# Layer 0 of a graph network: where the value sums live, when keys are asked for, and how many steps the next queries wait

## The chip, the cores and the metric

The kernel runs on one core of one Trainium2 chip. Its time is the time of one execution on the device in microseconds (us), the median of the runs. Smaller is better. The engines are TensorE (PE, with weight loads shown apart as PEld), VectorE (DVE), ScalarE (ACT), GpSimd (POOL) and SyncE (SP), whose queue issues nearly all transfers.

## The reference, cut to what matters

Four residual layers, each followed by a layer norm, run over 3327 nodes with 256 features and one adjacency matrix. The change touches layer 0 only:

```python
Qn = _cos_normalize(features @ Wq.T)          # x / max(|x|, 1e-4)
Kn = _cos_normalize(features @ Wk.T)
att = jnp.where(adj > 0, Kn @ Qn.T, NEG)
att = jax.nn.softmax(att, axis=1)
prop_fea = att @ features
...
x = _layernorm(x + _L0_gnn_ref(x, adj, Wq, Wk))
```

Layers 1 to 3 are graph attention layers of the same shape (masked scores, softmax, times values). The kernel runs them as five further passes over the same adjacency mask.

## The kernel before, in words

The nodes are padded to 3328, which is NT = 26 tiles of 128. One side of the attention matrix is cut into NB = 7 blocks of 512 columns (the last has 256). The other side is walked in 26 tiles. The main loop is a list of steps (layer, block b, tile j). In step j the loop makes the weights of a tile two steps ahead (`make_to`), and multiplies the weights of tile j with the values of tile j into accumulators `po`, which stand for the whole block.

To make one tile of weights in layer 0 (`weights0`), TensorE multiplies keys and queries into a PSUM bank `ps` (L455), ScalarE takes the exponential `ex` with the key's reciprocal length `rq` as its scale (L464), and VectorE multiplies by the mask into `e` (L444). Every second step also turns a pair of adjacency tiles into a mask (`take_adj`: ScalarE `pos` L407 and `mask` L408) and counts them (VectorE `acc` L416).

Block 0 uses plain products, eight matmul records of 257 columns in a step (L1271). Blocks 1 to 5 use a Strassen form (L726) that handles two tiles at once and needs sums of values. `combine` computes those sums in block 0, one pair of tiles p in step p + 9, with four VectorE subtractions (L656 to L659) and a column of ones set by GpSimd (L655). It writes them to DRAM with a transfer on SP (L660), and `fetch_tsum` streams them back for each later block (L664).

Keys come from `keys0`: a product `pq` (L305), then the square and a copy on ScalarE (L312, L313), then column sums `pn` on TensorE (L317), then the reciprocal root on VectorE (L322 and the lines of `rsqrt`). It is a generator, and one part of it runs in a step.

The queries of the next block come from `queries0(b + 1)`, also a part in a step: products `pk` (L335) and a copy (L343), then four squares with sums on ScalarE (L350), then `lengths` on GpSimd (L296 and `rsqrt`, 15 small instructions), then four scalings `kr` on ScalarE (L362), then four transposes `pkT` on TensorE (L366) and a copy (L367). In blocks 1 to 5 these parts are called in steps j = 10, 11, 12, 13 and 14; in block 0 in steps 18 to 22. The closing of the block before (`finish`) is spread over the first dozen steps of each block, most of it on VectorE.

The first four steps are emitted in written order on TensorE, ScalarE, VectorE and GpSimd. After that a scheduler sets the order of every engine: it plays the program through with modelled times, and an engine that is free in that play takes, among what is ready, the instruction that was written first. On the chip each engine keeps the order so found, and waits at the head of its queue for what is late.

Tiles come from rings of buffers. `x4k` (two buffers) holds `xT`, the pieces of the transposed input, and before the change also the sums of block 0. `tsum` (three buffers) holds the sums that come back. The PSUM banks for everything but `po` are a ring of three, and `e` has five.

Of the kernel before, what the change touches and what calls it, by code (L numbers as in the profile page):

```python
# [14 lines left out]
ALU = mybir.AluOpType  # L15
# [6 lines left out]
H = 128  # L22
# [5 lines left out]
COS_EPS = 1e-4  # L28
# [5 lines left out]
def gnn_stack(ctx: ExitStack, tc: tile.TileContext, a: dict, N: int, out: bass.AP):  # L34
# [8 lines left out]
    nc = tc.nc  # L43
# [6 lines left out]
    def bw(b):  # L50
        return min(CH, NP - b * CH)

    def tiles_of(b):
        return range(4 * b, min(4 * b + 4, NT))
# [11 lines left out]
    def bank(name):  # L66
        return ps_b.tile([P, CH], F32, tag="pb", name=name)
# [16 lines left out]
    n = 1  # L84
# [7 lines left out]
    for k in range(4):  # L92
# [5 lines left out]
    V = [  # L98
        [big.tile([P, D + 1], F32, name=f"v{i}_{t}") for t in range(NT)]
        for i in range(2)  # L100
    ]
# [30 lines left out]
    def rsqrt(dst, v, n, eng=nc.vector, tag="rs"):  # L132

        g = cols.tile([P, n], I32, tag=tag + "_g", name="rs_g")
        eng.tensor_scalar(g, v.bitcast(I32), -0.5, MAGIC, ALU.mult, ALU.add)
        y = g.bitcast(F32)
        vh = cols.tile([P, n], F32, tag=tag + "_v", name="rs_v")
        eng.tensor_scalar(vh, v, -0.5, None, ALU.mult)
        for k in range(3):
            q = cols.tile([P, n], F32, tag=tag + "_q", name="rs_q")  # L140
            eng.tensor_tensor(q, y, y, ALU.mult)
            eng.tensor_tensor(q, q, vh, ALU.mult)
            z = dst if k == 2 else cols.tile([P, n], F32, tag=tag + "_y", name="rs_y")
            if eng is nc.vector:
                eng.scalar_tensor_tensor(z, q, 1.5, y, ALU.add, ALU.mult)
            else:
                eng.tensor_scalar(q, q, 1.5, None, ALU.add)
                eng.tensor_tensor(z, q, y, ALU.mult)
            y = z
# [125 lines left out]
    def load_xT(g):  # L275
        wd = bw(g)
        xT = work.tile([P, 2, CH], F32, tag="x4k", name="xT", bufs=2)
        src = a["xT"].rearrange("(h p) n -> p h n", p=P)
        if g == 0:
            for q, c in ((nc.scalar, 0), (nc.sync, D)):  # L280
                q.dma_start(xT[:, :, c : c + D], src[:, :, c : c + D])
        else:
            nc.sync.dma_start(xT[:, :, :wd], src[:, :, g * CH : g * CH + wd])
        xTs[g] = xT

    def load_x(g):
        for t in tiles_of(g):
            nc.sync.dma_start(V[0][t][:, :D], a["x"][t * P : (t + 1) * P, :])
# [3 lines left out]
    rq = const.tile([P, NT], F32, name="rq")  # L292

    def lengths(dst, v, n, eng=nc.vector, tag="rs"):

        eng.tensor_scalar(v, v, COS_EPS * COS_EPS, None, ALU.max)  # L296
        rsqrt(dst, v, n, eng, tag)

    def keys0(g):

        wd, n = bw(g), len(tiles_of(g))
        xT = xTs[g]
        pm = bank("pq")
        for h in range(2):
            nc.tensor.matmul(  # L305
                pm[:, :wd], w["qk"][:, h, :H], xT[:, h, :wd], start=(h == 0), stop=(h == 1)
            )
            if g == 1 and h == 0:
                yield
        yield  # L310
        sq = work.tile([P, CH], F32, tag="u", name="qsq", bufs=2)
        nc.scalar.activation(sq[:, :wd], pm[:, :wd], AF.Square)  # L312
        nc.scalar.copy(FT[g][:, 0, :wd], pm[:, :wd])  # L313
        yield
        pn = bank("pn0")
        for k in range(n):
            nc.tensor.matmul(  # L317
                pn[:, k : k + 1], sq[:, k * P : (k + 1) * P], ones[:, :1], start=True, stop=True
            )
        yield  # L320
        v = cols.tile([P, 4], F32, tag="qss", name="qss")
        nc.vector.tensor_scalar(v[:, :n], pn[:, :n], COS_EPS * COS_EPS, None, ALU.max)  # L322
        rsqrt(rq[:, 4 * g : 4 * g + n], v[:, :n], n)

    def queries0(g):

        wd, n = bw(g), len(tiles_of(g))
        xT = xTs[g]
        ss = cols.tile([P, 4], F32, tag="kss", name="kss")
        kr = work.tile([P, 4, H], F32, tag="kr", name="kr", bufs=1)  # L330
        banks = [bank("pk") for _ in range(2 if g == 0 else 1)]
        for k in range(n):
            pk = banks[k // 2 if g == 0 else 0][:, k * H : (k + 1) * H]
            for h in range(2):
                nc.tensor.matmul(  # L335
                    pk,
                    xT[:, h, k * P : (k + 1) * P],
                    w["qk"][:, h, H:],
                    start=(h == 0),
                    stop=(h == 1),  # L340
                )
        if g > 0:
            nc.scalar.copy(kr.rearrange("p k n -> p (k n)")[:, :wd], banks[0][:, :wd])  # L343
            yield
        src = [
            banks[k // 2][:, k * H : (k + 1) * H] if g == 0 else kr[:, k, :] for k in range(n)
        ]
        for k in range(n):
            jk = work.tile([P, H], F32, tag="sq0", name="sq", bufs=1)
            nc.scalar.activation(jk, src[k], AF.Square, accum_out=ss[:, k : k + 1])  # L350
        yield
        rk = cols.tile([P, 4], F32, tag="rk", name="rk")
        if g == 0:
            lengths(rk[:, :n], ss[:, :n], n)
        else:
            lengths(rk[:, :n], ss[:, :n], n, nc.gpsimd, "prs")
        yield
        for k in range(n):
            if g == 0 and k >= 2:
                nc.vector.tensor_scalar(kr[:, k, :], src[k], rk[:, k : k + 1], None, ALU.mult)  # L360
            else:
                nc.scalar.mul(kr[:, k, :], src[k], rk[:, k : k + 1])  # L362
        yield
        pt = bank("pkT")
        for k in range(n):
            nc.tensor.transpose(pt[:, k * P : (k + 1) * P], kr[:, k, :], ident)  # L366
        nc.scalar.copy(FT[g][:, 1, :wd], pt[:, :wd])  # L367
# [273 lines left out]

    tsums = {}

    def combine(key, p, v):

        b1, b2 = v[2 * p], v[2 * p + 1]
        b11, b12, b21, b22 = b1[:, H:D], b1[:, :H], b2[:, H:D], b2[:, :H]
        here = key == "2" and p == NT // 2 - 1
        if here:
            t = work.tile([P, 4 * H + 1], F32, tag="tsum", name="tsums", bufs=3)  # L650
            tsums[0, p] = t
        else:
            t = work.tile([P, 4 * H + 1], F32, tag="x4k", name="tsum", bufs=2)
        t1, t2, t3, t4 = (t[:, c : c + H] for c in (0, H + 1, 2 * H + 1, 3 * H + 1))
        nc.gpsimd.memset(t[:, H : H + 1], 1.0)  # L655
        nc.vector.tensor_tensor(t1, b12, b11, ALU.subtract)  # L656
        nc.vector.tensor_tensor(t2, b22, t1, ALU.subtract)
        nc.vector.tensor_tensor(t3, b22, b12, ALU.subtract)
        nc.vector.tensor_tensor(t4, t2, b21, ALU.subtract)  # L659
        nc.sync.dma_start(t_d[key][p], t)  # L660

# [483 lines left out]
    def advance():  # L1145
        while pending:
            try:
                next(pending[0])
                return
            except StopIteration:  # L1150
                pending.popleft()
# [41 lines left out]
    make(0)  # L1193
    next(q1)
    make(1)
    prep = deque()
    kprep = iter(())
    setup = setups()
    pre = iter(())
# [5 lines left out]
    def make_to(n):  # L1205
        nonlocal upto
        while upto < n:
            make(upto)
            upto += 1

    for s, (L, b, j) in enumerate(steps):
# [9 lines left out]
        if first:  # L1221

            if j == 0:
                load_x(1)
                load_xT(2)
            elif j % 4 == 2 and j < 20:
                load_x((j + 6) // 4)
            elif j % 4 == 0 and j < 20:
                load_xT((j + 8) // 4)
        make_to(s + LA + 1 + extra)  # L1230
        if first:
            if j < 2:
                next(q1)
                if j == 1:
                    next(q1, None)
            elif j % 4 == 2 and j < 20:
                prep.append(keys0((j + 6) // 4))
            if prep:
                next(prep[0], None)
                if j % 4 == 0:  # L1240
                    next(prep.popleft(), None)
        if L.key == "0" and b < NB - 1:

            at = 14 if b == 0 else 6
            if j == at:
                load_xT(b + 1)
            elif j == at + 4:
                kprep = queries0(b + 1)
            if j >= at + 4:
                next(kprep, None)  # L1250
        es = None if end else made.popleft()
        if end:

            k, h = divmod(2 * j, NT)
# [27 lines left out]
        if L.key == "0" and j == NT - 1 - LA:  # L1282
            sum_adj(b)
        if first and 0 <= j - 9 < NT // 2:
            combine("0", j - 9, V[0])
        advance()
        if L.key == "0" and b < NB - 1:
            if j == 8:
# [104 lines left out]
```

## Time and profile before

| what | us |
|---|---|
| median of three runs | 2399.59 (2399.13 to 2400.09) |
| time of the profiled execution | 2401.12 |
| its span, first to last instruction | 2399.3 |
| TensorE busy in the span | 2357.4 |
| VectorE busy | 1607.1 |
| ScalarE busy | 1223.1 |
| GpSimd busy | 46.8 |

Layer 0 fills the first 470 us or so of the span. Block 0 ends at about 110 us, and blocks 1 to 5 take about 71 us each (with block 5 a little less). A line of the timeline is: start, duration, engine, line, operation, output and inputs, and in brackets how long the engine had been idle and what ended that idle time. A line of the waits is: who waited, for whom, total us, times, longest us. A line of the windows is: the stretch, its length, busy us of an engine with its number of instructions, the granted TensorE clock as a share of full speed, the share of DMA engines that were busy, and GB/s.

### The profile page before, as it was taken

The page shows a single profiled execution, that of the slowest core. Times are in us where ns is not written, and L with a number is a line of the kernel's source. Part 1 is how long each engine was busy: PE and PEld are TensorE (multiplying, and loading weights), DVE is VectorE, ACT ScalarE, POOL GpSimd, SP SyncE. Part 2 cuts the span into 40 slices and gives each one's busy share as a digit, 9 for nine tenths or more (in the row PEclk, how much of TensorE's full clock was granted, in tenths as well). Part 3 has the DMA queues.
Part 4 walks back from the last instruction along what each step waited for, and adds up shares of the span by engine and source line. Part 5 has one row for each costly group of instructions (what it writes and reads, how often), then busy time and mean ns, then how long its engine had stood idle before and what let it go on. Part 6 is the DMA issues. An engine that isn't in the chain of part 4 may idle for free.

```text
span 2399.3 us, 33184 instructions
## 1 busy us (share of the span) xinstructions
PE 2357.4 (98%) x11965; PEld 1920.3 (80%) x11965; DVE 1607.1 (67%) x4305; ACT 1223.1 (51%) x1952; POOL 46.8 (2%) x181
## 2 busy tenths in 40 slices
PE   9899999999999999999999999999999999999997
PEld 6677787888888867677677798888888888888886
DVE  6679898966666757566567586555656655655665
ACT  4566676665555522222222255555565555655554
POOL 0001101000000000000000000000000000000000
PEclk9999999999999999999999999999999999999999
DMA  7545555523322322122122131121121111132120
GB/s 258 180 162 169 176 184 186 180 70 101 91 73 52 88 80 80 47 86 86 40 86 72 42 126 51 46 71 35 44 78 42 42 45 56 47 101 69 60 64 23
DMA packets 147720, 215.45 MB, mean 90 GB/s; under 512 B 76141, under 2 KB 101220, under 8 KB 142948
## 3 DMA queue, kind: packets, MB, share of 16 engines
q1 hardware_dynamic: 147284, 213.07, 28.7%
q8 instruction: 94, 1.54, 0.3%
q14 instruction: 70, 0.57, 0.1%
q10 hardware_dynamic: 272, 0.26, 0.0%
HBM read 168.32 MB, written 28.19 MB: 82 GB/s over the span
## 4 chain that ended last, share of the span: by engine, by line
PE 87%; DVE 4%; DMA 3%; ACT 2%; issue 1%; POOL 1%; SPq 0%; POOLq 0%; DVEq 0%; ACTq 0%
PE po L1271 46%; PE po L726 17%; PE ps L519 12%; PE ps L455 4%; PE pproj L935 3%; DMA stage<-in_adj_a 1%; DMA turned<-planes 1%; PE pv L1020 1%; PE pgq L478 1%; ACT re L613 1%; PE po L1256 1%; POOL kss L296 0%; DVE ejunk L547 0%; DVE e L444 0%; DVE acc L416 0%
## 5 line engine op out<-in xcount | busy, mean ns | idle before, releaser
L1271 PE MATMUL po<-v,e 128*128 128x257 f32 x5616 | 1252.1, 381 | 1.3 <-ACT p L904 1.3
L1271 PEld LDWEIGHTS po<-v,e 128*128 128x128 f32 x5616 | 1063.1, 190 | 169.7 <-issue 11.6
L613 ACT ACTIVATE re<-u,nrh,th 128x512 f32<-128x512 f32 (+1 forms) x728 | 555.9, 780 | 477.7 <-DVE e L624 474.1
L624 DVE SCALAR_TENSOR_TENSOR e<-re,rh,mask 128x512 f32<-128x512 f32 (+1 forms) x702 | 502.1, 719 | 378.9 <-PE po L1271 357.0
L444 DVE SCALAR_TENSOR_TENSOR e<-ex,mask 128x512 f32<-128x512 f32 (+1 forms) x364 | 235.1, 648 | 208.5 <-ACT ex L527 158.0
L519 PE MATMUL ps<-gT,ft 128*128 128x512 f32 (+1 forms) x728 | 307.4, 563 | 0.0
L527 ACT ACTIVATE ex<-ps,off 128x512 f32<-128x512 f32 (+1 forms) x182 | 119.3, 656 | 360.0 <-PE ps L519 333.4
L726 PE MATMUL po<-tsums,ssum 128*128 128x128 f32 (+1 forms) x1794 | 250.8, 276 | 0.5 <-DVE ssum L676 0.3
L726 PEld LDWEIGHTS po<-v,e 128*128 128x128 f32 x1196 | 171.4, 193 | 69.6 <-issue 54.6
L726 PEld LDWEIGHTS po<-tsums,ssum 128*128 128x128 f32 x1794 | 225.4, 192 | 2.1 <-DVE ssum L676 1.5
L519 PEld LDWEIGHTS ps<-gT,ft 128*128 128x128 f32 x728 | 132.0, 190 | 114.5 <-issue 111.7
L726 PE MATMUL po<-v,e 128*128 128x129 f32 x1196 | 184.3, 277 | 0.1
L464 ACT ACTIVATE ex<-ps,rq 128x512 f32<-128x512 f32 (+1 forms) x182 | 118.8, 653 | 117.8 <-PE ps L455 110.2
L455 PE MATMUL ps<-ft,ft 128*128 128x512 f32 (+1 forms) x312 | 145.7, 571 | 2.1 <-ACT w L252 1.8
L416 DVE CUSTOM_DVE_ANT_0 acc<-acc,stage 128x1024 uint16<-128x1024 uint16 (+1 forms) x168 | 108.4, 645 | 11.8 <-DMA stage<-in_adj_a 9.3
L726 PE MATMUL po<-v,ssum 128*128 128x128 f32 x598 | 92.3, 275 | 0.0
L726 PE MATMUL po<-tsums,e 128*128 128x128 f32 x598 | 92.1, 275 | 0.0
L408 ACT ACTIVATE mask<-pos 128x1024 uint8<-128x1024 bf16 (+1 forms) x87 | 86.3, 992 | 2.3
L407 ACT ACTIVATE pos<-stage 128x1024 bf16<-128x1024 int32 (+1 forms) x87 | 85.5, 983 | 0.0
L935 PE MATMUL pproj<-w_l_w,pT 128*128 128x256 f32 x304 | 78.0, 381 | 2.9 <-DVE pT L791 2.6
L726 PEld LDWEIGHTS po<-v,ssum 128*128 128x128 f32 x598 | 79.4, 192 | 0.1
L726 PEld LDWEIGHTS po<-tsums,e 128*128 128x128 f32 x598 | 79.3, 192 | 0.0
(241 smaller groups left out, 1744.9 us busy)
## 6 DMA issues: line engine op xcount, KB each, us to landing
mask<-mask_d SPq DMA_DIRECT2D x30, 1664.0 KB
stage<-in_adj_a SPq DMA_DIRECT2D x78, 512.0 KB
tsums<-t_d SPq DMA_DIRECT2D x155, 256.5 KB
mask_d<-mask SPq DMA_DIRECT2D x6, 1664.0 KB
t_d<-tsum SPq DMA_DIRECT2D x25, 256.5 KB
u<-s_d SPq DMA_DIRECT2D x24, 256.0 KB
xT<-in_xT SPq DMA_DIRECT2D x10, 512.0 KB
mask<-mask_d SPq DMA_DIRECT2D x5, 832.0 KB
```

Source lines behind the costliest of these rows:

```text
L408: nc.scalar.activation(mask(b, j, 2), t_[:, : 2 * wd], AF.Sign)
L416: nc.vector.tensor_tensor(acc, acc, st[:, h * wd : (h + 1) * wd], ALU.add)
L444: nc.vector.scalar_tensor_tensor(e[:, :wd], t_[:, :wd], 0.0, mask(b, j), ALU.add, ALU.mult)
L455: nc.tensor.matmul(ps[:, :wd], FT[j // 4][:, 0, (j % 4) * P : (j % 4 + 1) * P], FT[b][:, 1, :wd], start=True, stop=True,)
L464: nc.scalar.activation(t_[:, :wd], ps[:, :wd], AF.Exp, scale=rq[:, j : j + 1])
L519: nc.tensor.matmul(ps[:, :wd], FT[j // 4][:, h, (j % 4) * P : (j % 4 + 1) * P], g[:, h, :wd], start=(h == 0), stop=(h == 1),)
L527: nc.scalar.activation(t_[:, :wd], ps[:, :wd], AF.Exp, bias=off, scale=1.0 / D**0.5)
L613: nc.scalar.activation(t_[:, :wd], self.u[b][:, :wd], AF.Relu, bias=self.nrh[:, j : j + 1], scale=self.th[:, j : j + 1],)
L624: nc.vector.scalar_tensor_tensor(e[:, :wd], t_[:, :wd], self.rh[:, j : j + 1], mask(b, j), ALU.add, ALU.mult,)
L726: nc.tensor.matmul(o, x, y, start=(p == 0 and g not in banks[:i]), stop=(p == NT // 2 - 1 and g not in banks[i + 1 :]),)
L935: nc.tensor.matmul(pm[:, :D], pT[:, h, :], w[L.w][:, h, :], start=(h == 0), stop=(h == 1),)
L1271: nc.tensor.matmul(pos[k], es[:, k * P : (k + 1) * P], V[L.i % 2][j], start=(j == 0), stop=(j == NT - 1),)
```

## The change

Four edits, all in layer 0.

1. `combine` in block 0 takes its buffer from the `tsum` ring and no longer from `x4k`. It gets the tile `e` of its own step. The column of ones is now computed on VectorE as "the first column of e is at least 0" (which is always true), and two of the four subtractions become scalar-tensor-tensor instructions that read this column as a scalar. So they can't run before `e` exists.
2. `keys0` is started at j = 2, 5, 9, 13 and 17 (before: 2, 6, 10, 14 and 18), and its input `xT` is asked for at j = 3, 7, 11 and 15 (before: 4, 8, 12 and 16). Before, the last two of its four parts fell in one step; now each has its own, but for the first.
3. The column sums `pn` are copied out of PSUM by ScalarE, and the maximum is then taken in place by VectorE (`lengths`).
4. `queries0` starts at j = 6 in blocks 1 to 5 and at j = 13 in block 0 (before: 10 and 18). Between `lengths` and the scalings there are five steps where there was one, and the scalings are spread over two steps. The parts then fall in steps 6, 7, 8, 13, 14 and 15 (block 0: 13, 14, 15, 20, 21 and 22).

```diff
--- before.py
+++ after.py
@@ -319,8 +319,8 @@
             )
         yield
         v = cols.tile([P, 4], F32, tag="qss", name="qss")
-        nc.vector.tensor_scalar(v[:, :n], pn[:, :n], COS_EPS * COS_EPS, None, ALU.max)
-        rsqrt(rq[:, 4 * g : 4 * g + n], v[:, :n], n)
+        nc.scalar.copy(v[:, :n], pn[:, :n])
+        lengths(rq[:, 4 * g : 4 * g + n], v[:, :n], n)
 
     def queries0(g):
 
@@ -354,8 +354,12 @@
             lengths(rk[:, :n], ss[:, :n], n)
         else:
             lengths(rk[:, :n], ss[:, :n], n, nc.gpsimd, "prs")
+            for _ in range(4):
+                yield
         yield
         for k in range(n):
+            if g > 0 and k == 2:
+                yield
             if g == 0 and k >= 2:
                 nc.vector.tensor_scalar(kr[:, k, :], src[k], rk[:, k : k + 1], None, ALU.mult)
             else:
@@ -641,21 +645,29 @@
 
     tsums = {}
 
-    def combine(key, p, v):
+    def combine(key, p, v, e=None):
+
 
         b1, b2 = v[2 * p], v[2 * p + 1]
         b11, b12, b21, b22 = b1[:, H:D], b1[:, :H], b2[:, H:D], b2[:, :H]
         here = key == "2" and p == NT // 2 - 1
-        if here:
+        if here or key == "0":
             t = work.tile([P, 4 * H + 1], F32, tag="tsum", name="tsums", bufs=3)
-            tsums[0, p] = t
         else:
             t = work.tile([P, 4 * H + 1], F32, tag="x4k", name="tsum", bufs=2)
+        if here:
+            tsums[0, p] = t
         t1, t2, t3, t4 = (t[:, c : c + H] for c in (0, H + 1, 2 * H + 1, 3 * H + 1))
-        nc.gpsimd.memset(t[:, H : H + 1], 1.0)
-        nc.vector.tensor_tensor(t1, b12, b11, ALU.subtract)
+        if e is None:
+            nc.gpsimd.memset(t[:, H : H + 1], 1.0)
+            nc.vector.tensor_tensor(t1, b12, b11, ALU.subtract)
+            nc.vector.tensor_tensor(t3, b22, b12, ALU.subtract)
+        else:
+            one = t[:, H : H + 1]
+            nc.vector.tensor_scalar(one, e[:, :1], 0.0, None, ALU.is_ge)
+            nc.vector.scalar_tensor_tensor(t1, b12, one, b11, ALU.mult, ALU.subtract)
+            nc.vector.scalar_tensor_tensor(t3, b22, one, b12, ALU.mult, ALU.subtract)
         nc.vector.tensor_tensor(t2, b22, t1, ALU.subtract)
-        nc.vector.tensor_tensor(t3, b22, b12, ALU.subtract)
         nc.vector.tensor_tensor(t4, t2, b21, ALU.subtract)
         nc.sync.dma_start(t_d[key][p], t)
 
@@ -1193,7 +1205,7 @@
     make(0)
     next(q1)
     make(1)
-    prep = deque()
+    prep = iter(())
     kprep = iter(())
     setup = setups()
     pre = iter(())
@@ -1225,28 +1237,27 @@
                 load_xT(2)
             elif j % 4 == 2 and j < 20:
                 load_x((j + 6) // 4)
-            elif j % 4 == 0 and j < 20:
-                load_xT((j + 8) // 4)
+            elif j % 4 == 3 and j < 16:
+                load_xT((j + 9) // 4)
         make_to(s + LA + 1 + extra)
         if first:
             if j < 2:
                 next(q1)
                 if j == 1:
                     next(q1, None)
-            elif j % 4 == 2 and j < 20:
-                prep.append(keys0((j + 6) // 4))
-            if prep:
-                next(prep[0], None)
-                if j % 4 == 0:
-                    next(prep.popleft(), None)
+            elif j == 2 or j % 4 == 1 and j < 18:
+                prep = keys0(max(2, (j + 7) // 4))
+            next(prep, None)
+            if j == 4:
+                next(prep, None)
         if L.key == "0" and b < NB - 1:
 
-            at = 14 if b == 0 else 6
+            at = 10 if b == 0 else 3
             if j == at:
                 load_xT(b + 1)
-            elif j == at + 4:
+            elif j == at + 3:
                 kprep = queries0(b + 1)
-            if j >= at + 4:
+            if j >= at + 3:
                 next(kprep, None)
         es = None if end else made.popleft()
         if end:
@@ -1282,7 +1293,7 @@
         if L.key == "0" and j == NT - 1 - LA:
             sum_adj(b)
         if first and 0 <= j - 9 < NT // 2:
-            combine("0", j - 9, V[0])
+            combine("0", j - 9, V[0], es)
         advance()
         if L.key == "0" and b < NB - 1:
             if j == 8:
```

## The prediction

> **What bounds the kernel now.** I read the page's busy times first, then who waited for whom in layer 0 (36 to 440 us, TensorE, then ScalarE), then the timeline around the longest waits.
>
> ```profile
> PE 2357.4 (98%) x11965; PEld 1920.3 (80%) x11965; DVE 1607.1 (67%) x4305; ACT 1223.1 (51%) x1952; POOL 46.8 (2%) x181
> ...
> PE pkT L366 <- ACT kr L362: 11.9, 7, 3.6
> PE pq L305 <- DMA xT<-in_xT: 3.2, 1, 3.2
> PE ps L455 <- ACT w L252: 1.8, 1, 1.8
> PE pasum L431 <- DVE af L427: 0.6, 1, 0.6
> PE po L726 <- DVE ssum L676: 0.3, 1, 0.3
> PE ps L455 <- ACT ex L464: 0.3, 1, 0.3
> ...
> ACT kr L362 <- POOL rk L148: 26.5, 5, 5.9
> ```
>
> TensorE is the bound: of 2399.3 us it idles 42, and layer 0 has some 18 of them in few places. One is a late `xT`; nearly all others lead to the scaled queries `kr`, which wait on ScalarE for roots from GpSimd. Block 2 shows how:
>
> ```profile
> 217.54 0.30 ACT L350 ACTIVATE sq<-kr 128x128 f32<-128x128 f32 x1
> ...
> 218.02 3.48 POOL L296 TENSOR_SCALAR kss<-kss 128x4 f32<-128x4 f32 x1 [67.49 <-ACT sq L350]
> ...
> 225.45 0.40 ACT L362 ACTIVATE kr<-kr,rk 128x128 f32<-128x128 f32 x1 [5.88 <-POOL rk L148]
> 225.76 0.67 ACT L464 ACTIVATE ex<-ps,rq 128x512 f32<-128x512 f32 x1
> 225.90 0.14 PEld L366 LDWEIGHTS pkT<-ident,kr 128*128 128x128 f32 x1 [3.07 <-ACT kr L362]
> 225.91 0.33 PE L366 MATMUL pkT<-ident,kr 128*128 128x128 f32 x1 [2.24 <-ACT kr L362]
> ```
>
> From the last square to the roots it is 7.6 us (217.84 to 225.45). Not only the transposes wait: the scaling stands ahead of an exponential in ScalarE's queue, whose input `ps` was done at 219.5.
>
> Windows, TensorE for the first two, then VectorE:
>
> ```profile
> 76.40:79.60 3.20, 0.02 (x1) 1.00 0.55 173
> 79.60:86.20 6.60, 6.58 (x29) 0.74 0.21 81
> ...
> 199.00:209.00 10.00, 10.00 (x37) 1.00 0.51 158
> ...
> 218.00:226.00 8.00, 3.41 (x7) 1.00 0.54 174
> ...
> 427.00:436.00 9.00, 7.24 (x17) 1.00 0.50 171
> ```
>
> A stall costs twice: after the 3.2 us idle the granted clock is 0.74 for 6.6 us, 1.7 us more. And VectorE is full in steps 6 to 9 of block 2 (199 to 209), but not when the roots run now.
>
> One line of layer 1 says how far a written step binds:
>
> ```profile
> 745.92 0.51 ACT L605 ACTIVATE u<-u,ub 128x256 f32<-128x256 f32 x1 [2.29 <-DMA u<-s_d]
> ```
>
> Only the last block is 256 wide. Its `u` is written six steps after its load, in step 20 of block 5; with a pitch of 52.2 us (block 2 ends at 652.06) that is about 795. It ran 50 us earlier, and ScalarE stood 2.3 us for it. So extra `yield`s give an instruction a lower rank, not a time.
>
> [...] here 2.24 + 0.54 us were enough (0.76 from 225.9 to 233), while the 1.82 us in block 1 were not. [...] the 14 root instructions after L296 take 3.85 us in block 2, but 6.2 in block 5, where VectorE is 80% busy. [...] in block 0 L296 starts 6.7 us after its squares (86.5 to 93.25).
>
> **The change part by part**, against the profiled span of 2399.3 us.
>
> *The ring.* Six `xT` loads shared two buffers with 13 sums. The load that stalled was issued at 76.72, just when a write of sums issued at 74.06 had landed. In the ring of three only `xT` is left in `x4k`, and the last piece can be issued when `pk` of step 13 has freed its buffer, four steps or some 12 us before its use; it needs 2.9 (76.72 to 79.62). Gain: 3.2 + 1.7 = 4.9. The three fetches that used the `tsum` ring at 44 to 56 us now come after the last sums, step 21 or later. They are needed from step 1 of block 1, 10 us or more later, against a write and a read of some 3 us each. Nothing.
>
> *The sums* cost VectorE 13 x (0.16 for the column + 2 x 0.06) = 3.6 us: 0.16 is its smallest row, and 0.06 is what the same form costs more with a column scalar (L624 719 ns, L444 648, 512 wide). GpSimd's memsets go. But the 13 sums were spread from 38.8 to 98 us, and now want steps 9 to 21. A step there is 3.2 us of TensorE (2.59 + a quarter of 1.72 + 0.79 for keys), and VectorE has e 0.65 + acc 0.69 + sums 1.3 + roots 0.58 = 3.2. It is level. SP's writes stand ahead of its adjacency loads, so lateness would pass on to `acc` and `e`. I bound the loss by 0 and 8 us (13 x 0.6, if each step ran at 3.8) and take 2.
>
> *Keys a step sooner, and the copy.* The same instructions plus six copies on ScalarE at about 0.24 (as L593), which is half idle. At the start the copy stands behind the copy at 12.24, so the first `rq` comes at 15.6 instead of 13.7; the exponential waits for `ps` until 15.43, so 0 to 0.3 us; I take 0. Without that cover it costs 1.9.
>
> *Queries.* Block 0: the transposes stay in step 22 and the roots start five steps sooner. They need 12.4 us now (86.5 to 98.9) and five steps are 16, so the stall of 3.58 us and 1.7 of clock (0.71 from 99.4 to 105.3), 5.3, goes, even if a full VectorE stretches the roots by 2.4 as in block 5. Blocks 1 to 5: the transposes move to seven steps (17 us) after `lengths` and never wait. What remains is ScalarE's queue. The sequence there was: exponential, scaling, exponential. With the lower rank the pair `pos`, `mask` of the next tiles (2.1 us) and the next exponential can go first, so I expect the first scaling about 3 us after its last place. But the roots now run beside the full VectorE: 3.55 (L296, with the gap after it) + 6.2 = 9.7 us, where it was 7.6. So ScalarE would stand for some 5 us, and the weights two steps on would be late by 0 (roots in 7.6) to 2.5 (in 9.7). Before, one such block lost 2.8 + 1.7 = 4.5. I take 1.5 left: 3 x 3.0 = 9.0 gained in blocks 2 to 4. In block 1 of 1.8 I take 0.8 (no long L296 there: 0.26), in block 5 nothing.
>
> Sum: 4.9 + 5.3 + 9.0 + 0.8 - 2 = 18.0. The span becomes 2381.3, the profiled execution 2383.1 (it lies 1.8 above its span). The median lies 1.5 below the profiled execution: 2381.6, say 2382.
>
> **The rivals.**
>
> *All of it* (0.12): the scalings drop behind two pairs of `pos` and `mask`, or L296 loses its 3.2 us of start. It had them after pauses of 64 us or more, not after 60 and 47, and shorter blocks shorten the pause. Then 4.9 + 5.3 + 1.8 + 3 x 4.5 = 25.5, less 1: 2375.
>
> *The yields don't hold on ScalarE* (0.22): the scaling still stands ahead of the next exponential, as L605's place suggests. The transposes no longer wait, but the products do: in block 2 they would be reached at 224.4, with their weights ready at 227.1. So 2.3 us idle (the first products need only the even tile) and 1.7 of clock remain at 7.6 us of roots, and 6.1 in all at 9.7. Blocks 2 to 4 then give between +0.5 and -1.6 each, and with 4.9 + 5.3 - 2 the time is 2390 to 2397; I take 2393. That is the edit not doing what it says.
>
> *Slower* (0.21): the same place, and roots at 0.6 us an instruction beside a full VectorE, 3.5 + 8.4 = 11.9 us. Each us over 7.6 is one more idle us: 2.8 + 4.3 + 1.7 = 8.8 for 4.5 in blocks 2 to 4 (+13), and block 1 with 8.7 for 4.8 us of roots +4. Against 8.2 gained in block 0: 2408. It decides from about 10 us of roots. For it: VectorE is 10.00 of 10 busy there[...]. Against: only the first 5 us of the roots fall into the full stretch, and 3.5 of these are L296.
>
> **How the numbers follow.** Forecast 0.45 at 2382 (own range 2377 to 2388), and the rivals as above. The range of 2372 to 2400 holds all but the slower case. A measurement of this kernel can't tell 0.2% (4.8 us) from no change. Faster: 0.45 + 0.12 + 0.13 of the second rival = 0.70. Same: its other 0.09 and 0.01 of the slower case = 0.10. Slower: 0.20.
>
> **What the profile would show.** Right: no wait of `pq` for `xT`; no wait of `pkT` for `kr`; ScalarE's wait at L362 for roots below 5 us; granted clock 1.00 through block 0 after 20 us; TensorE idle in blocks 2 to 4 below 2 us each. Wrong: products L726 that wait for `e` or `ssum` in steps 9 to 13; root chains over 10 us; `acc` waiting longer for adjacency loads than the 8.9 us of now, or products L1271 waiting for `e` in block 0.

## The result, and the profile after

The changed kernel takes 2385.36 us (median of six runs, 2384.84 to 2386.15); the kernel before took 2399.84 (2397.4 to 2400.68) beside it. The ratio is 0.9942, with a 95% interval from 0.9929 to 0.9954, so it is faster by 0.46 to 0.71%. The profiled execution took 2385.32 us and its span is 2383.5, 15.8 less than before. The forecast was 2382 for the median and 2381.3 for the span.

The page's busy times after:

```profile
PE 2349.8 (99%) x11965; PEld 1916.8 (80%) x11965; DVE 1609.4 (68%) x4318; ACT 1222.2 (51%) x1959; POOL 42.1 (2%) x168
```

TensorE does the same 11965 instructions in 7.6 us less (2357.4 before), most of it work at half clock that is gone (in each of blocks 2 to 4 the granted clock was 0.98 on average over 70 us before, about 1.4 us lost, and is 1.00), and its idle time falls from 42 to 33.7. The two together are the 15.8.

The waits of layer 0 (36 to 440 us) after: who waited, for whom, total us, times, longest.

```profile
PE pasum L435 <- DVE af L431: 5.1, 2, 4.4
PE po L738 <- DVE e L448: 1.8, 1, 1.8
PE po L738 <- DVE ssum L688: 1.2, 3, 0.6
PE ps L459 <- ACT ex L468: 0.9, 1, 0.9
PE po L1282 <- issue: 0.5, 1, 0.5
...
ACT kr L366 <- POOL rk L148: 22.3, 6, 5.6
...
DVE acc L420 <- DMA stage<-in_adj_a: 10.4, 6, 3.2
```

The waits for `xT` and for `kr` are gone, 15 us of them. One large wait is new: `pasum`, the transposes that close the count of edges of a block, waits for `af`. ScalarE still waits 22 us for roots, but that time no longer reaches TensorE in blocks 0 to 4.

Block 2 in the timeline after:

```profile
205.31 0.19 ACT L350 ACTIVATION_READ_ACCUMULATOR sq<-kr 128x1 f32 x1
...
205.59 0.34 POOL L296 TENSOR_SCALAR kss<-kss 128x4 f32<-128x4 f32 x1 [67.33 <-ACT sq L350]
...
205.78 0.07 DVE L551 DVE_READ_ACCUMULATOR2_ANT sd<- 128x1 f32 x1
...
205.99 0.69 ACT L468 ACTIVATE ex<-ps,rq 128x512 f32<-128x512 f32 x1 [0.48 <-PE ps L459]
...
206.84 0.69 ACT L468 ACTIVATE ex<-ps,rq 128x512 f32<-128x512 f32 x1 [0.17 <-PE ps L459]
...
207.43 1.05 ACT L411 ACTIVATE pos<-stage 128x1024 bf16<-128x1024 int32 x1
...
210.71 0.51 POOL L148 TENSOR_TENSOR rk<-rs_q,rs_y 128x4 f32<-128x4 f32 x1
...
211.25 0.40 ACT L366 ACTIVATE kr<-kr,rk 128x128 f32<-128x128 f32 x1 [2.78 <-POOL rk L148]
...
221.61 0.60 PE L370 MATMUL pkT<-ident,kr 128*128 128x128 f32 x4
```

From the end of the last square (205.50) to the first scaling it is 5.7 us, not 7.6 as before and not the 9.7 of the forecast: L296 takes 0.34 us where it took 3.48. Two exponentials and a `pos` stand ahead of the scaling, and the transposes come ten us later without any wait.

The end of block 0, where the new wait is (SP's queue, VectorE, TensorE):

```profile
88.70 4.49 SPq L676 DMA_DIRECT2D tsums<-t_d  x2
...
93.28 0.38 SPq L400 DMA_DIRECT2D stage<-in_adj_a  x1
...
93.72 0.42 SPq L890 DMA_DIRECT2D mask_d<-mask  x1
...
97.90 1.42 DVE L420 CUSTOM_DVE_ANT_0 acc<-acc,stage 128x1024 uint16<-128x1024 uint16 x2 [3.24 <-DMA stage<-in_adj_a]
...
99.84 0.42 DVE L431 CAST af<-acc 128x512 f32<-128x512 int32 x1
...
100.40 1.08 PE L435 MATMUL pasum<-ident,af 128*128 128x128 f32 x4 [4.44 <-DVE af L431]
```

The input of `af` is block 0's count, and the last addition to it ended at 80.66. But the `acc` at 97.90 belongs to block 1 (the program's order on VectorE tells the two counts apart), stands ahead of `af` in VectorE's queue, and waits for an adjacency load. Windows of TensorE after (stretch, length, busy us, granted clock, DMA share, GB/s):

```profile
95.00:100.00 5.00, 0.96 (x5) 0.83 0.97 366
100.00:105.00 5.00, 4.60 (x11) 0.50 0.43 177
...
180.00:250.00 70.00, 69.94 (x473) 1.00 0.61 200
250.00:320.00 70.00, 69.94 (x468) 1.00 0.58 192
320.00:390.00 70.00, 69.94 (x467) 1.00 0.56 187
```

Blocks 2 to 4 have no idle time left (0.06 of 70 us) and the full clock. The clock falls during the stall at the end of block 0, and the 5 us after it still run at half clock.

Where the 15.8 us came from is read best at a fixed point of each block, the start of `pasum` in step 23. The first column is when TensorE reached it, that is its start less its wait.

| kernel | reached | wait | block 1 | blocks 2, 3, 4 | block 5 | `pasum` of block 5 |
|---|---|---|---|---|---|---|
| before | 105.24 | 0 | 75.84 | 71.15, 71.39, 71.44 | 67.08 | 462.14 |
| after | 95.96 | 4.44 | 77.94 | 66.20, 66.20, 66.19 | 68.74 | 445.67 |

Block columns are the distance from one `pasum` to the next. So block 0 gave 9.3 us and gave 4.4 of them back, block 1 lost 2.1, blocks 2 to 4 gave 15.4, and block 5 lost 1.7: 16.5 in all at this point, 15.8 at the end.

### The profile page after: what moved, and what is told of

It is laid out like the page before. It is cut to its first block, busy times and chain, and to the rows that moved or that the text cites. A ratio compares the mean times of both kernels' runs of the same rounds, so it can differ in the third digit from the quotient of the medians.

```text
span 2383.5 us, 33176 instructions
## 1 busy us (share of the span) xinstructions
PE 2349.8 (99%) x11965; PEld 1916.8 (80%) x11965; DVE 1609.4 (68%) x4318; ACT 1222.2 (51%) x1959; POOL 42.1 (2%) x168
## 4 chain that ended last, share of the span: by engine, by line
PE 88%; DVE 7%; ACT 2%; DMA 2%; issue 1%; POOL 0%; POOLq 0%; SPq 0%; DVEq 0%; ACTq 0%
PE po L1282 48%; PE po L738 16%; PE ps L523 12%; PE ps L459 4%; PE pproj L947 3%; DVE e L448 1%; PE pv L1032 1%; PE pgq L482 1%; DVE acc L420 1%; DVE ejunk L551 1%; DMA turned<-planes 1%; PE po L1267 1%; ACT re L617 1%; DMA stage<-in_adj_a 1%; PE pq L305 1%
## 5 line engine op out<-in xcount | busy, mean ns | idle before, releaser
L1282 PEld LDWEIGHTS po<-v,e 128*128 128x128 f32 x5616 | 1063.2, 190 | 169.3 <-issue 10.9
L420 DVE CUSTOM_DVE_ANT_0 acc<-acc,stage 128x1024 uint16<-128x1024 uint16 (+1 forms) x168 | 108.5, 646 | 14.7 <-DMA stage<-in_adj_a 10.9
```

What stands on the lines that cost most here:

```text
L420: nc.vector.tensor_tensor(acc, acc, st[:, h * wd : (h + 1) * wd], ALU.add)
L1282: nc.tensor.matmul(pos[k], es[:, k * P : (k + 1) * P], V[L.i % 2][j], start=(j == 0), stop=(j == NT - 1),)
```

## The experiments

All ratios are to the kernel before, run on the same chip beside each kernel; the median of before was 2400.5, 2404.4, 2402.9 and 2400.1 us in the four groups, so ratios and spans are compared, not medians. A span is that of one execution, the one that the traces show: it lies 2 to 4 us above the median of its kernel in the runs with edit 1 alone and with edit 4 undone, and as much below it in the run without extra steps, the run with all roots on VectorE and the last one. The kernel after was not run again in these groups, and in the second and third group every kernel looks 2 to 6 us better against it by the ratio than by the span. So a difference of a few us between two changed kernels is not shown by their times alone; the lengths of blocks and the waits, read from the traces, show more. "Theory" in the expectations is what I held at the time.

**Edit 1 alone.**

```diff
-            combine("0", j - 9, V[0])
+            combine("0", j - 9, V[0], es)
```

with the new `combine` (ring of three, column on VectorE), and nothing else of the change.

> The kernel before with edit 1 alone (sums of block 0 in the ring of three, tied to their step by the weights). Theory: three things follow. The six pieces of the transposed input have their two buffers to themselves, so pq no longer waits for xT (3.2 us and 1.7 of half clock, -4.9). GpSimd has no memsets ahead of its first root instruction, so its start-up is over in the first microseconds and not at 86 us; the roots of block 0 take some 5.5 us instead of 12.4 and the transposes of block 0 no longer wait (3.58 and 1.7, -5.3). The fetches of sums now stand behind the last writes of sums on SP, ahead of adjacency loads, and pasum at the end of block 0 waits 4.4 us and loses some 2 of clock (+6.5). Blocks 2 to 4 as before. Together -3.7: about 2396. Rival 1 (the loss of edit 1 is the 2 us of the forecast, and the wait of pasum has to do with the queries): -8.2, about 2391.5. Rival 2 (the late start of the first roots is not owed to the memsets): +1.6, about 2401.

Measured: 2390.88 us, ratio 0.9959 (0.9945 to 0.9973), span 2392.5. TensorE reached `pasum` at 94.96 and waited 2.20; blocks 2 to 4 took 71.4 us each, as before. The instructions of L296 on GpSimd (shortest, median and longest ns; first and last start), then TensorE's waits:

```profile
L296 POOL TENSOR_SCALAR kss<-kss x6: 223/1894/3513, 81.4 to 421.0; 128x4 f32<-128x4 f32 x5, 128x2 f32<-128x2 f32 x1
L296 POOLq MODIFY_POOL_CONFIG  x2: 6/6/6, 3.0 to 3.1; - x2
```

```profile
PE pkT L366 <- ACT kr L362: 8.3, 6, 2.2
PE pasum L431 <- DVE af L427: 2.2, 1, 2.2
PE ps L455 <- ACT w L252: 1.8, 1, 1.8
```

The transposes of block 0 don't wait any more, though the queries stand in their old steps. The first instruction of L296, `MODIFY_POOL_CONFIG`, ran at 3.0 us; in the kernel before it stood behind the memsets of sums and ran at 86.4:

```profile
L296 POOLq MODIFY_POOL_CONFIG  x2: 11/11/11, 86.4 to 86.4; - x2
```

In the run with edit 4 alone, which keeps the memsets, it follows one too, at 61.9 us. L296 itself starts 0.1 us after the last square here (81.30 to 81.41), 6.1 us after it with edit 4 alone (64.90 to 71.03), and 6.7 in the kernel before. What takes these 6 us is not shown. So the 10.3 us that block 0 gained (105.24 to 94.96) are those that the prediction put at 4.9 + 5.3, but edit 1 alone brings both. The median came out near the first rival's 2391.5, but the wait of `pasum` is there without the new queries, at 2.2 us and not at the theory's 4.4.

**Edit 4 alone.**

```diff
-            at = 14 if b == 0 else 6
+            at = 10 if b == 0 else 3
...
-            elif j == at + 4:
+            elif j == at + 3:
```

with the four extra steps and the split scalings.

> The kernel before with edit 4 alone (queries started earlier, five steps for the roots). Theory: blocks 2 to 4 lose their stall before the transposes, 5.0 to 5.2 us each as between the two traces (-15.5), block 5 gets 1.7 longer; in block 0 the five steps cover the roots, late start-up of GpSimd included (-5.3), while the wait for xT stays (0) and no wait of pasum comes up. Together -19: about 2381, less than with all four edits. Rival (edit 4 needs the ring, since the memsets on GpSimd and the xT of the next queries stand in the same two buffers and are now asked for in the midst of the sums): block 0 gains nothing or loses up to 5, blocks 2 to 4 as said, -9 to -14: 2386 to 2391.

Measured: 2384.74 us, ratio 0.9934 (0.9920 to 0.9947), span 2383.1. As much as all four edits give. TensorE reached `pasum` at 96.89 and waited 1.95, blocks 2 to 4 took 66.20, 67.39 and 66.81, block 5 70.72. Blocks 2 to 4 gave 13.6 us where the theory had 15.5, and block 5 lost 3.6 where it had 1.7. The theory was wrong in that the wait for `xT` would stay (it is gone too) and that `pasum` would not wait. Edits 1 and 4 both remove block 0's stalls, so their gains don't add: 9.6 and 15.8 us singly, 14.5 with all four edits, by the medians. The wait of `pasum` comes up here without the ring, so the ring's fetches are not its only cause.

**The extra steps taken out.**

```diff
-            for _ in range(4):
-                yield
         yield
         for k in range(n):
-            if g > 0 and k == 2:
-                yield
```

> The kernel after with the four extra steps between the roots and the scalings taken out again and the scalings in one step; the early start (step 6) stays. Theory (the early start shortens the roots, because their first instruction no longer falls into an unbroken run of VectorE, and the extra steps only keep the transposes out of the way): roots stay at 5.7 us, the transposes stand right behind the next products and wait 0.6 + 0.5 us, the first pair of pos and mask stands behind the scalings: +1.1 to 1.5 in each of blocks 1 to 4 and no half clock, about +5: 2390. Rival (the extra steps carry the gain): the stall of 4.5 is back in blocks 2 to 4, +13.5 to 15.5: about 2400.

Measured: 2387.59 us, ratio 0.9944 (0.9931 to 0.9957), span 2382.0; the kernel after has 0.9942 and 2383.5. From the timeline of block 2, and the windows of TensorE:

```profile
198.83 0.34 POOL L296 TENSOR_SCALAR kss<-kss 128x4 f32<-128x4 f32 x1 [66.10 <-ACT sq L350]
...
204.49 1.28 ACT L362 ACTIVATE kr<-kr,rk 128x128 f32<-128x128 f32 x4 [3.72 <-POOL rk L148]
...
204.94 1.21 PE L366 MATMUL pkT<-ident,kr 128*128 128x128 f32 x4 [0.92 <-ACT kr L362]
```

```profile
95.00:100.00 5.00, 2.14 (x10) 1.00 0.93 374
```

The roots are as short as in the kernel after, 0.34 us for L296 included, and each of blocks 2 to 4 takes 67.55 us in place of 66.20: the extra steps are worth 1.35 a block, 4 us in three. The early start brings the other 3.6 to 3.9. In the span even the 4 us don't show, because this execution came through the end of block 0 without half clock, though its `pasum` waited 3.59 us, and its block 1 took 73.75 in place of 77.94. Its time is 3.8 us below the median of six, with the highest mean clock of them (0.998; the others 0.996 or 0.997), so what this trace shows of the end of block 0 need not hold for the others.

**Edit 4 undone, the rest kept.** The old steps and a single step for the roots.

> The kernel after with edit 4 undone (queries in their old steps, one step for the roots); the ring, the keys and the copy stay. Theory: in blocks 2 to 4 the first root instruction takes 3.5 us again and the stall before the transposes is back (+15.5), block 5 gets its 1.7 back, and in block 0 the transposes hardly wait, since GpSimd's start-up now lies in the first microseconds. Together +14: about 2399, no better than the kernel before. Rival (the ring shortens the roots in all blocks, for instance because GpSimd's memsets are gone): 2386.

Measured: 2396.23 us, ratio 0.9983 (0.9976 to 0.9989), span 2397.2. Blocks 2 to 4 took 72.28, 69.88 and 73.34, block 5 66.68, and block 0's transposes did not wait. The theory held for the blocks; in all the kernel took 10.9 us longer than the kernel after by the medians, not 14. L296 is long again, and its end is telling (block 4; GpSimd, the last VectorE instruction of an unbroken run, GpSimd's next):

```profile
357.24 3.64 POOL L296 TENSOR_SCALAR kss<-kss 128x4 f32<-128x4 f32 x1 [63.30 <-ACT sq L350]
...
360.11 0.69 DVE L416 CUSTOM_DVE_ANT_0 acc<-acc,stage 128x1024 uint16<-128x1024 uint16 x1
...
360.97 0.19 POOL L135 TENSOR_SCALAR rs_g<-kss 128x4 int32<-128x4 int32 x1
```

It ends at 360.88, 0.08 us after VectorE's run (360.80). In block 2 of this kernel it started 0.18 us later against that run and took 3.47 (214.31 to 217.78, run's end 217.69); in block 2 of the run with edit 1 alone 3.51 (ends 214.32 and 214.24). The kernel before shows the same in blocks 2 to 4 (L296 ends at 221.50, 292.62 and 364.01, the run at 221.41, 292.53 and 363.93): whatever its start, L296 ends 0.08 to 0.09 us after a run of additions and products with two inputs each. The other three long cases, blocks 3 and 4 with edit 1 alone and block 3 with edit 4 undone, took 3.47 us each. In the kernel after VectorE is just as full there, but its run holds summed products L551, each followed by a read of the accumulator of 0.07 us, and L296 ends 0.08 us after such a read in each of blocks 2 to 4 (205.93 and 205.85 in block 2). Why L296 ends there and not sooner is not shown: in block 1 of the kernel after it ends at 133.02, 0.07 us after one VectorE addition, though the next addition had begun at 132.86 without a break. No run here changes VectorE's run alone.

**Edits 2 and 3 undone, edits 1 and 4 kept** (keys in their old steps, the maximum straight from PSUM).

> The kernel after with edits 2 and 3 undone (keys and their inputs at the old steps, maximum on VectorE straight from PSUM); the ring and the queries of edits 1 and 4 stay. The two runs with old queries, with and without edits 2 and 3, stood 5.3 us apart. Theory: edits 2 and 3 cost about as much here, part of it a longer wait of pasum (3.4 against 2.2 us there): about 2380, pasum waits 2 to 3 us. Rival (the forecast: these edits are worth nothing, and the 5.3 us came from one wait of 1.8 or 1.9 us falling on either side of what lowers the clock): 2385.

Measured: ratio 0.9928 (0.9915 to 0.9940), 2386.30 us, span 2384.8, 1.3 more than after. The intervals overlap, the spans point the other way: nothing that I can measure, as forecast. `pasum` waited 5.42 us here, so the theory of a shorter wait is refuted, and beside the new queries these edits have no such price. Of the 5.3 us between the two runs with old queries, 2.5 are in block 1 (79.29 with edit 4 undone, 76.75 with edit 1 alone): in the first, TensorE's wait of 1.9 us was followed by a lower clock (0.83 from 150 to 160 us); in the second, a wait of 1.8 us was not (1.00 there).

**The sums without their tie to the weights.**

```diff
-            combine("0", j - 9, V[0], es)
+            combine("0", j - 9, V[0])
```

> The kernel after with the sums of block 0 as they were (column of ones by GpSimd, plain subtractions, no tie to the weights of their step), but in the ring of three. Theory (the tie is there to keep the scheduler from taking the sums early, since they need only the values): without it the first sums stand on VectorE ahead of the first roots and weights and wait there for the first values, so the start is 2 to 5 us later; but the last sums are written out long before the end of block 0, the fetches don't stand on SP, and the wait of pasum (4.4) with its half clock (2) goes: -4 to -1, 2381 to 2384. Rival (the tie costs nothing and saves nothing but memsets): 2385; pasum waits as in the kernel after.

Measured: ratio 0.9914 (0.9901 to 0.9928), 2383.86 us, span 2382.3. The theory held in the main: the first products start 1.8 us later (20.21 against 18.45), since VectorE waits 2.4 us for the first values ahead of its first roots; TensorE reaches `pasum` only at 100.19, but waits there 0.51. By the spans it is 1.2 us better than the kernel after, by the ratios more; that the tie helps is not shown.

**Four buffers for the sums.** In both places of the ring `bufs=3` becomes `bufs=4`.

> The kernel after with four buffers in the ring of sums in place of three. Theory (the new wait of pasum at the end of block 0 comes from SP, which stands some 4 us at fetches of sums whose buffer is still being written out, with adjacency loads behind them): the fetches find a free buffer, the adjacency loads are issued up to 4 us earlier, pasum waits 2 us or less in place of 4.4, and the half clock after it (0.74 from 100 to 110 us) goes: -4 to -6, about 2380. Rival (the adjacency loads are late because block 0 has become shorter than its transfers, whatever stands ahead of them): no change, 2385.

Measured: ratio 0.9934 (0.9921 to 0.9948), 2387.74 us, span 2384.9. `pasum` waited 5.41: no gain. It didn't test the theory, because a fourth fetch moved up in SP's queue and waited for the last write in place of the third (4.80 us at 89.04).

**The last two sums in the other ring.**

```diff
-        if here or key == "0":
+        if here or key == "0" and p < 11:
```

> The kernel after with the last two sums of block 0 in the ring that holds the transposed input, which has no user left by then; the ring of sums keeps its three buffers. With four buffers a fourth fetch moved up on SP and waited for the last write in place of the third, so that run didn't test the theory. Here the three fetches stand ahead of the last two writes and need only buffers that were written out earlier. Theory (the adjacency load that pasum waits for stands on SP behind a fetch that waits for the last write): SP no longer stands 4.5 us, the load issued at 93.28 goes out 3 to 5 us earlier, pasum waits under 1.5 us in place of 4.4, no half clock from 100 to 110: -4 to -6, ratio to the kernel before about 0.992. Rival (the transfers of the end of block 0, 97% of the DMA engines' time from 95 to 100 us, are the limit whatever their order): pasum waits 3 us or more, ratio 0.994.

Measured: ratio 0.9935 (0.9922 to 0.9949), 2386.74 us, span 2384.5. SP and VectorE at the end of block 0:

```profile
90.58 0.47 SPq L400 DMA_DIRECT2D stage<-in_adj_a  x1
91.14 0.38 SPq L890 DMA_DIRECT2D mask_d<-mask  x1
...
97.08 1.42 DVE L420 CUSTOM_DVE_ANT_0 acc<-acc,stage 128x1024 uint16<-128x1024 uint16 x2 [3.00 <-DMA stage<-in_adj_a]
```

The load goes out 2.7 us earlier (93.28 after), and comes in 0.8 earlier: 6.5 us where it was 4.6. It now shares the DMA engines with an `xT` load issued at 90.15 and with the 1664 KB of the mask (DMA share 0.92 from 90 to 95 us and 1.01 from 95 to 100), and `pasum` still waits 3.60. So SP's queue is not what sets the wait; the rival, the transfers, held.

**All roots of the next queries on VectorE.**

```diff
-            lengths(rk[:, :n], ss[:, :n], n, nc.gpsimd, "prs")
+            lengths(rk[:, :n], ss[:, :n], n)
```

> The kernel after with the roots of all next queries on VectorE in place of GpSimd (11 instructions for 15), the extra steps kept. Theory (GpSimd's 5.5 to 7 us per block cost TensorE nothing in blocks 2 to 4, which have no idle time left, and some 1.7 us in block 5, where ScalarE waits 5.6 us for them): blocks 2 to 4 unchanged at 66.2 us, block 5 shorter by 1.7 to 2.7, other blocks within 1: about 2383. Rival (VectorE is full in steps 6 to 9, so its own roots, about 1 us a block, delay e and the sums of weights by as much): up to +1 in each of five blocks, 2385 to 2390.

Measured: ratio 0.9909 (0.9895 to 0.9922), 2382.71 us, span 2377.6, better than the kernel after by both. Two of its waits in layer 0:

```profile
PE po L738 <- DVE ssum L688: 1.7, 3, 0.6
...
ACT kr L366 <- DVE rk L145: 1.7, 3, 0.8
```

(The roots are 12 instructions a block on VectorE, not the 11 of the expectation: the page counts 4390 of VectorE's, 72 more than after, in six blocks.) ScalarE's wait for roots falls from 22.3 to 1.7 us. Block 5 takes 66.23 in place of 68.74, as the theory had it; blocks 2 to 4 take 66.8 to 67.0, 0.6 to 0.8 more, and there TensorE waits 0.6 for `ssum` once a block: the rival's price, at the lower end.

**Both.** The last two sums in the other ring, and VectorE's roots where they pay:

```diff
-        if g == 0:
+        if g in (0, 1, 2, NB - 1):
             lengths(rk[:, :n], ss[:, :n], n)
```

> The kernel after with the last two sums in the other ring as in the run before it, and the roots of the queries of blocks 1, 2 and 6 (made in blocks 0, 1 and 5) on VectorE; those made in blocks 2 to 4 stay on GpSimd, since there VectorE's roots cost 0.6 us a block. Theory: the two add up. Roots on VectorE gave 2.5 in block 5 and some 2 in block 0 and block 1 apart from pasum; with 4 to 6 from the wait of pasum that is -9 to -11 against the kernel after: ratio about 0.990, blocks 2 to 4 at 66.2 us each. Rival (block 0 is bound by its transfers, so that what the roots free is waited for at pasum): only block 5's 2.5 and block 1's half clock are left, ratio 0.992.

Measured: ratio 0.9895 (0.9877 to 0.9913), 2377.62 us, span 2376.7. Blocks 2 to 4 66.2 each, block 5 66.56, `pasum` waits 2.22. As the theory said by the ratio; by the span it is 6.8 better than the kernel after.

**The mask's write held back.**

```diff
+            nc.vector.tensor_scalar(
+                masks[b][:, :1], masks[b][:, :1], c2[:, :1], None, ALU.min
+            )
             nc.sync.dma_start(mask_d[b], masks[b][:, : NT * wd])
```

> The kernel after with the write of block 0's mask to DRAM (1664 KB, issued at 93.72, 0.44 us after the adjacency load that VectorE waits for) held back until pasum is through, by one small instruction on the mask's first column that reads a value made from pasum (the minimum of 0 or 1 and a value of 1.5 or more, so the mask stays as it is). The same in blocks 1 to 6. The load issued at 93.28 took 4.6 us to acc at 97.90, others about 2.7, and that acc, which belongs to block 1, stands ahead of e and af of block 0 in VectorE's queue. Theory (the 1664 KB share the DMA engines with that load, 0.97 busy from 95 to 100): the load lands 1.5 to 2 us earlier, pasum waits 2.5 to 3 us in place of 4.4, less half clock after it: -2 to -4, ratio to the kernel before 0.993. Rival (the load is held up by the fetches of sums and by its late issue alone): pasum waits 4 us or more, ratio 0.994 to 0.995, or worse, since the next adjacency loads now stand behind the held-back write on SP.

Measured: ratio 0.9930 (0.9916 to 0.9944), 2384.56 us, span 2382.4. The load took 3.6 us (92.30 to `acc` at 95.91) in place of 4.6, a gain of 1.0 us where the theory asked for 1.5 to 2, though the next adjacency load was now issued right behind it. `pasum` waits 3.66 us, between the theory and its rival. The ratio is the theory's; by the span it is 1.1 us, too little to tell.

**The three together, and a buffer of its own for `af`.**

```diff
-        af = work.tile([P, CH], F32, tag="e", name="af", bufs=5)
+        af = work.tile([P, CH], F32, tag="af", name="af", bufs=1)
```

> The best kernel so far (last two sums in the other ring, roots for blocks 1, 2 and 6 on VectorE; ratio 0.9895) with the mask's write held back as in the run before, and with a buffer of its own for af, which so far shares the ring of weights and so comes late in VectorE's queue, behind acc of block 1. Theory: af is made some 15 us before pasum wants it, pasum doesn't wait; the products after it may wait up to 2 us for the weights that stand behind the same acc. -2 to -4: ratio 0.988 to 0.989, 2373 to 2376 where the kernel before takes 2400. Rival (the stall only moves from pasum to the products behind it, with the same length, since the acc of block 1 stands ahead of these weights all the same): ratio 0.9895.

Measured: 2373.53 us, ratio 0.9885 (0.9867 to 0.9903), span 2369.5: the best kernel of this study, 14.0 us of span below the kernel after (11.8 by the medians). `af` and `pasum` in its timeline, then TensorE's waits from 36 to 440 us:

```profile
76.13 0.42 DVE L431 CAST af<-acc 128x512 f32<-128x512 int32 x1
...
92.68 0.60 PE L435 MATMUL pasum<-ident,af 128*128 128x128 f32 x4
```

```profile
PE pkT L370 <- ACT kr L366: 1.3, 1, 1.3
PE po L738 <- DVE e L448: 1.0, 1, 1.0
PE po L738 <- DVE y L780: 0.3, 1, 0.3
```

`af` is made 16.6 us before it is wanted, `pasum` has no wait and the clock stays at 1.00 from 85 to 115 us. `acc` of block 1 still waits 2.65 us for its load (93.04), and the products behind it don't wait: TensorE is busy for all 30 us from 85 to 115. The load still comes after TensorE has reached `pasum` (92.68), and `pasum` doesn't wait. So the late load stalled TensorE only through the order on VectorE, where `af` stood behind the next block's `acc`. As I read the program, it stood there because it shared the ring of weights and could be written only when an old weight was used up. The rival, that the stall would move to the products, is refuted. What the buffer of `af` brings without the other edits was not run apart.

## Why the prediction was right, and where its terms were off

*The ring, 4.9.* Right: no `pq` waits for `xT`, and with edit 1 alone block 0 gains that and the next term.

*Block 0's queries, 5.3.* The size was right (block 0 gained 9.3 with the term before, where the two were 10.2), the reason one of two. I credited the five steps of edit 4. Edit 1 alone does it as well, by taking the memsets from ahead of `MODIFY_POOL_CONFIG`, which then lies at 3.0 us and not at 86.4, with L296 0.1 us and not 6.7 after the last square. I had the late start of L296 in block 0 before me, and the memsets named as "go", and didn't join them.

*Blocks 2 to 4, 9.0.* Measured 15.4 (4.95, 5.19 and 5.25). The term that was mis-sized is the root chain: 9.7 us by the forecast, 5.7 measured, so that no stall was left where I took 1.5 a block. That makes 4.5 a block; the 0.6 or so that each block gave beyond it is not explained. The step that failed is the price of L296. I took 3.55 over from before and tied it to GpSimd's pauses of 64 us or more. Its pause in block 2 after is 67.33 us, and it takes 0.34; with edit 4 undone it takes 3.64 after a pause of 63.30. So the pause doesn't set it. That what VectorE runs at that moment does, fits the ends of L296 in blocks 2 to 4 but was not tested alone. That GpSimd would be slower beside the full VectorE was right only for some instructions (0.53 the longest in block 2).

*The place of the scalings.* Predicted behind a pair of `pos` and `mask` and another exponential; they stand behind two exponentials and the `pos`. The prediction rested on these extra steps. They are worth 1.35 us a block (the run without them); the early start, with its shorter roots, brings the other 3.6 to 3.9. The rival in which they do not hold on ScalarE is refuted, and so is the slower one: the chain never came near 10 us there.

*Block 1, 0.8 gained.* Measured 2.1 lost. The wait of 1.82 us is gone, but the half clock after the stall of `pasum` falls into it: 4.60 busy us at 0.50 are 2.3 us. Smaller waits (0.8 us for `ssum` among them) take the old wait's place, so TensorE idles only 0.9 us less there, and 0.6 us more of busy time are not explained.

*Block 5, nothing.* Measured 1.7 lost. Two scalings stand so early that ScalarE waits 5.6 us for them; with the roots on VectorE block 5 took 66.23.

*Keys and copy, 0.* Nothing that I can measure, as the run without edits 2 and 3 shows.

*The loss, 2 (0 to 8).* Measured 4.4 at `pasum`, and the 2.3 us of half clock in block 1 with it. The sign that the prediction named came: `acc` waits 10.4 us for adjacency loads, 8.9 before. But the way is another than "VectorE is level". VectorE was busy 49.49 of 74 us from 36 to 110. The transfers of a shorter block 0 come late, and an early `acc` of the next block carries that to `af`.

The prediction came out close because a gain that was 6.4 us too small (blocks 2 to 4) met losses that were 7 too small: 4.4 + 2.1 + 1.7 at `pasum` and in blocks 1 and 5, where I had 2 lost and 0.8 gained. That two errors cancelled is luck. The rest is block 0's gain, 9.3 where I had 10.2, and 0.7 after block 5. Two of the signs of being right failed: the clock did not stay at 1.00 through block 0, and ScalarE's wait for roots reached 5.6 us in block 5. The rival "All of it" had the right event, L296 losing its start, for a wrong reason.

## What to carry to other kernels

When an edit removes a stall, ask what now comes next on each queue: here a shorter block 0 ran into its own transfers, through an instruction of the next block that stood in front. Two edits that cover the same stall don't add, so run each alone; one of the four gave the whole gain here. A small instruction on GpSimd has no fixed price beside VectorE (L296 took 0.34 or 3.48 us): look at what VectorE runs at that moment. Look also whether the tail of a block shares a ring that holds it back.

## What was not expected of the hardware

The granted clock after a wait is not a matter of the wait's length alone. At the end of block 0, a wait of `pasum` of 3.59 us left the clock at 1.00 (the run without extra steps), while waits of 1.95 to 3.60 gave a mean of 0.87 from 94 to 107 us, and 3.66 to 5.42 gave 0.74. The means fall on these three values in all eleven kernels with such a wait, in steps of one stretch of about 3.4 us at half clock (0.13 x 13 us is 1.7, or half of 3.4). The window of the kernel after, and that of the run without extra steps:

```profile
94.00:107.00 13.00, 8.56 (x28) 0.74 0.63 230
```

```profile
94.00:107.00 13.00, 9.41 (x44) 1.00 0.63 235
```

In the first TensorE was busy 8.56 us with 28 instructions, in the second 9.41 with 44. Shorter windows show the stretches themselves, first in the kernel after, then in the run with edit 4 alone:

```profile
98.00:98.50 0.50, 0.00 (x0) 0.79 1.00 426
98.50:105.00 6.50, 4.60 (x11) 0.50 0.57 240
105.00:105.50 0.50, 0.50 (x3) 0.89 0.00 0
```

```profile
99.00:99.50 0.50, 0.50 (x5) 0.89 1.54 426
99.50:102.50 3.00, 3.00 (x6) 0.50 0.83 246
102.50:103.00 0.50, 0.50 (x3) 0.70 0.98 385
```

Worked out from the shares of the outer windows, the half clock lasts 6.8 us in the first, beginning 2.3 us into the wait of 4.44, and 3.4 us in the second, beginning 0.6 us after the wait of 1.95 had ended. Why nearly equal waits end differently (3.59 us with the clock at 1.00, 3.60 with a mean of 0.87) is not shown; a wait of 1.95 us was enough for one stretch.

VectorE's roots on 128 x 4 elements show 0.15 to 0.16 us each in the trace, but a block with 12 of them more was only 0.6 to 0.8 us longer: they overlap with their neighbours (203.42 and 203.49 are the starts of two of them in block 2 of the run with all roots on VectorE).
